# Layers 1 and 2 values by seven block products in a four-layer graph-attention stack, with the mask of layer 0 added out of PSUM

## The chip, the cores and the metric

The kernel runs on one core of one Trainium2 chip. The metric is the device time of one execution in microseconds (us). Three runs of the kernel before gave 2368.14, 2368.44 and 2372.44 us, the median is 2368.44 us.

## What is computed

The input is `x`, 32 graphs of 512 nodes with 256 features, and `adj`, a 0/1 adjacency of 512 x 512 for each graph. All is fp32. Four layers follow one another; each normalises its input, applies a graph attention, and adds the result back. Graphs are independent of one another.

```
for every layer:  h = relu(layernorm(x));  x = x + layer(h)
layer 0: s = (h att_W) h^T / 16 + mask(0 or -1000);  A = softmax(s)
         y = tanh(A (h W0 + b0));  out = tanh(A (y W1 + b1))
layer 1: Wh = h W^T;  e = leaky(Wh a1 [rows] + Wh a2 [columns]);  masked softmax;  out = A Wh
layer 2: Hh = h W;  e = exp(-leaky(s + d)) * (adj != 0);  out = elu(e Hh / rowsum)
layer 3: g = h W;  logits = g a12 g^T + g a1 + g a2;  leaky, masked softmax;
         out = elu(h W1 + A h W2)
```

"Values" in what follows are the rows that the attention averages: h W0 in layer 0, Wh in layer 1, Hh in layer 2, h W2 in layer 3. In layers 1 and 2 the two score columns (Wh a1 and Wh a2) are computed together with the values, as two further columns of the weights.

## The kernel before

**A graph as a list of operations.** A graph has 512 nodes: 4 tiles of 128 rows (NT = 4). `graph(b, ...)` does not emit instructions; it lists operations (`op`), each with an engine, a cost out of the table at L38 to L50, the operations it comes after, and the tiles that it uses. `Plan.order` (L131) is a list scheduler that runs all 32 lists through a simulation with due times. It fixes one order for each engine and gives the tiles their places: 34 SBUF pages (`PAGES`), 8 PSUM banks, 5 value buffers, 3 planes buffers, and `FLIGHT` slots, one for each graph in work. `SLACK` (L67) stretches the costs of VectorE, ScalarE and the DMAs in that simulation. `Plan.best` tries several spacings of the graphs' due times and keeps the one whose replay ends first. On the chip each engine then runs its list strictly in order, with semaphores where one engine needs another.

**One layer in the list.** `normed` (L521) computes mean and variance of each row on VectorE (L526, L527, L530), the reciprocal root on POOL (L533), the normed rows on ScalarE (L540). Then the rows are transposed by DMA: the fp32 words are split into two planes of 16 bits by a copy on VectorE (`split`, L545), the planes are turned by a DMA (L548), and a copy on ScalarE (`join`, L560) puts the halves back together as hT (features on partitions). Only layer 0 of graph 0 is turned by TensorE.

**Products.** In layers 0 (from graph 1 on) and 3 most products are made by a scheme of seven block products in place of eight (`seven`, L586). The operands are cut into 2 x 2 blocks; sums of blocks are formed on VectorE by `block_sums` (L618: four sums of 128 x 256 for each operand that isn't a weight; the sums of weights are made once by `seven_of`, L388). Each of the seven products then accumulates into a bank that is read out part by part: a product is added onto what the bank holds, a block is written out by one engine (`write`), the next product is added onto it, and three blocks get a further term by VectorE (`add`). So TensorE may enter the next product of a bank only when the block before has been read out. In layers 1 and 2 the values are made plainly by `scored_values` (L649): for each tile of 128 nodes, two products with 258 columns (2 scores and 256 values), and a copy out by ScalarE (L662). In the trace each fp32 product appears as two matmul records, so a layer has 4 tiles x 2 x 2 = 16 such records a graph.

**Scores of layer 0.** The seven products `q0` (L833) are read out by ScalarE (L847; the block (1,0) directly by the exponential, L841), added to by VectorE (L850), exponentiated by ScalarE (L841), and multiplied by `mask0` on VectorE (L856). `mask0` is 1 for an edge and 2^-100 for none (L516).

**Attention.** `attend` (L711) multiplies the weights e by the values, with a column of ones behind the values that yields the row sum: L721, 16 steps of 2 records for each pair of tiles, 257 columns in layers 0 to 2 and 259 in layer 3. Layers 1 to 3 add the result to x on VectorE: L929 in layer 1, and in layer 2 L962 and L966 for each tile of 128 x 256. Layer 0 has its own second product (L878, L896) and adds the result to x by L907.

Of the kernel before, what the change touches and what calls it, by code (L numbers as in the profile page):

```python
# [25 lines left out]
LEAST = 2.0**-126  # L26
LOWEST = -3.0e38
# [25 lines left out]
class Plan:  # L53
# [13 lines left out]
    SLACK = {"V": (1.05, 0.0), "A": (1.05, 0.0), "G": (1.5, 0.0), "D": (1.0, 800.0)}  # L67
# [138 lines left out]
def kernel(  # L206
# [36 lines left out]
    FLIGHT = 5  # L243
    PAGES, VALUES = 34, 5
    TURNED = 2
    LEAD = 2
# [105 lines left out]

    def transposed(w_sb, dst, after, *keys):
        done = []
        for c in range(HC):
            key = f"bank{next(banks)}"

            def turn(c, key):
                for r in range(HC):
                    nc.tensor.transpose(W[key][:, r * P : (r + 1) * P], w_sb()[:, r, c * P : (c + 1) * P], ident)  # L360

            def out_of(c, key):
                nc.vector.tensor_copy(dst()[:, c, :], W[key][:, : HC * P])

            a = prepare("PE", pe(nt=HC), after, partial(turn, c, key), key, *keys)
            done.append(prepare("V", V_ADD, [a], partial(out_of, c, key), key, *keys))
        return done
# [41 lines left out]
    l1_aug, l2_aug = (tile_of(n, H + 2) for n in ("l1_aug", "l2_aug"))  # L409
# [5 lines left out]
    for n, dst, w, key in (("w0", w0_s, w0, "raw9"), ("att", att_s, att_w, "raw10")):  # L415
# [9 lines left out]
    l3_wide = raw("raw8", H + 2)  # L425
    a = [load(l1_sb, rows_of(l1_w), "raw0")]
    ready["l1"] = transposed(l1_sb, lambda: l1_aug[:, :, 2:], a, "raw0")
    a += [load_column(l1_ac, l1_a.rearrange("n o -> (n o)"))]
    ready["l1"] += product(lambda d: l1_aug[:, d, 0:2], l1_sb,
                           lambda c: l1_ac.rearrange("p (o c) -> p c o", o=2)[:, c, :], 2, a, "raw0")  # L430
    a = [load(l2_aug[:, :, 2:], rows_of(l2_w))]
    a = ready["l2"] = a + transposed(lambda: l2_aug[:, :, 2:], l2_wt, a, "raw1")
    a = a + [load_column(l2_ac, l2_a.rearrange("o n -> (o n)"))]
    ready["l2"] = a + product(lambda d: l2_aug[:, d, 0:2], l2_wt,
                              lambda c: l2_ac.rearrange("p (o c) -> p c o", o=2)[:, c, :], 2, a, "raw1")
# [25 lines left out]
    def graph(b, adj_before, x_before):  # L461
# [53 lines left out]
        def mask0():  # L515
            nc.vector.tensor_scalar(T["mask0"], T["codeT"], HUGE, TINY, ALU.is_equal, ALU.max)  # L516
# [4 lines left out]
        def normed(l, xs):  # L521
# [21 lines left out]
            def split(t):  # L543
                bits = T[f"xn{l}"][:, t, :].bitcast(U16).rearrange("p (h b) -> p b h", b=2)
                nc.vector.tensor_copy(T[f"planes{l}_{t}"], bits)  # L545
# [18 lines left out]
            for g in range(NT // 2):  # L564
# [7 lines left out]
                for t in (2 * g, 2 * g + 1):  # L572
                    flat, over = f"planes{l}_{t}", f"planesT{l}_{t}"
                    a = op("A", A_NORM, [r], partial(norm, t), "x", f"xn{l}")
                    if b == l == 0:

                        key = f"bank_n{t}"
                        a = op("PE", pe(nt=2 * HC), [a], partial(turn_pe, t, key), f"xn{l}", key)
                        done.append(op("V", V_ADD, [a], partial(out_of, t, key), f"hT{l}", key))
                        continue  # L580
                    a = op("V", V_SPLIT, [a], partial(split, t), f"xn{l}", flat)
                    a = op("D", D_TURN, [a], partial(turn, t), flat, over)
                    done.append(op("A", A_JOIN, [a], partial(join, t), over, f"hT{l}"))
# [34 lines left out]
        def block_sums(dst, source, b, after, left):  # L618
# [16 lines left out]
            one = op("V", V_SUM, after, partial(form, 1), dst, source)  # L635
            three = op("V", V_SUM, after, partial(form, 3), dst, source)
# [12 lines left out]
        def scored_values(l, hs, w_aug, ready):  # L649

            cols = w_aug.shape[2]
            vs = []
            for t in range(NT):
                key = f"bank_v{l}{t}"

                def product(t, key):
                    for c in range(HC):
                        nc.tensor.matmul(T[key][:, :cols], T[f"hT{l}"][:, c, t * P : (t + 1) * P],  # L658
                                         w_aug[:, c, :], start=(c == 0), stop=(c == HC - 1))

                def values(t, key):
                    nc.scalar.copy(T[f"v{l}"][:, t, :cols], T[key][:, :cols])  # L662

                a = op("PE", pe(n258=4), [hs[t]] + ready, partial(product, t, key), key, f"hT{l}")
                vs.append(op("A", A_HALF, [a], partial(values, t, key), key, f"v{l}"))
            return vs

        def leaky_exp_t(l, vs, sign):
# [24 lines left out]
            def leaky(c):  # L693
                row = T[key] if turned else T[key][:, 0, :]
                nc.scalar.activation(e(l, c), row, AF.Prelu, bias=T[v][:, c, 1:2], alpha=ALPHA)  # L695
# [15 lines left out]
        def attend(l, es, vs, use):  # L711
# [3 lines left out]
            lead = LEAD if l < 3 else 0  # L715
# [12 lines left out]
            return done  # L728

# [80 lines left out]
        else:  # L810
# [29 lines left out]
            def exp0(i, l, key=None):  # L840
                nc.scalar.activation(block_e0(i, l), two_tiles(key, 0, N // 2) if key else block_e0(i, l), AF.Exp,  # L841
                                     scale=float(H) ** -0.5)

            def write_q(i, l, key, start, after):
                if (i, l) == (1, 0):
                    return op("A", A_COPY, after, partial(exp0, i, l, key), key, f"e0_{l}")
                return op("A", A_COPY, after, lambda: nc.scalar.copy(block_e0(i, l), two_tiles(key, 0, N // 2)), key, f"e0_{l}")  # L847

            def add_q(i, l, key, start, after):
                a = op("V", V_MASK, after, lambda: nc.vector.tensor_tensor(  # L850
                    block_e0(i, l), block_e0(i, l), two_tiles(key, 0, N // 2), ALU.add), key, f"e0_{l}")
                exps.append(op("A", A_EXP, [a], partial(exp0, i, l), f"e0_{l}"))
                return exps[-1]

            def masked0(i, l):
                nc.vector.tensor_tensor(block_e0(i, l), block_e0(i, l), T["mask0"][:, two(l), half(i)], ALU.mult)  # L856

            exps = []
            qb = seven("q0", pe(n256=4), lambda x, right_after=right_after, left_after=left_after: right_after(x) + left_after(x),
                       ("hT0", "hs0", "fa0", "fs0"), partial(scores0, right, left), write_q, add_q)  # L860
            es = {il: op("V", V_MASK, [a, m0], partial(masked0, *il), "mask0", f"e0_{il[1]}") for il, a in qb.items()}
# [27 lines left out]
        for g in range(NT // 2):  # L889
# [16 lines left out]
            def add_z(t):  # L906
                nc.vector.tensor_add(T["x"][:, t, :], T["x"][:, t, :], T["z0"][:, t, :])  # L907
# [4 lines left out]
            xs += [op("V", V_ADD, [a], partial(add_z, 2 * g + j), "z0", "x") for j in range(2)]  # L912
# [6 lines left out]
        vs = scored_values(1, hs, l1_aug, ready["l1"])  # L919
# [3 lines left out]
        def second(t, a, key):  # L923
            def sums():
                nc.vector.reciprocal(T["rs1"][:, t : t + 1], T[key][:, H : H + 1])

            def add():
                xt = T["x"][:, t, :]
                nc.vector.scalar_tensor_tensor(xt, T[key][:, :H], T["rs1"][:, t : t + 1], xt, ALU.mult, ALU.add)  # L929
# [8 lines left out]
        vs = scored_values(2, hs, l2_aug, ready["l2"])  # L938
# [7 lines left out]
        def third(t, a, key):  # L946
            def sums():
                rs = T["rs2"][:, t : t + 1]

                nc.vector.tensor_scalar(rs, T[key][:, H : H + 1], LEAST, None, ALU.max)  # L950
                nc.vector.reciprocal(rs, rs)


            def lower():
                nc.scalar.activation(T["y2"][:, t, :], T[key][:, :H], AF.Exp, scale=T["rs2"][:, t : t + 1])

            def upper():
                nc.scalar.activation(T["r2"][:, t, :], T[key][:, :H], AF.Relu, scale=T["rs2"][:, t : t + 1])

            def add_lower():  # L960
                xt = T["x"][:, t, :]
                nc.vector.scalar_tensor_tensor(xt, T["y2"][:, t, :], 1.0, xt, ALU.min, ALU.add)  # L962

            def add_upper():
                xt = T["x"][:, t, :]
                nc.vector.scalar_tensor_tensor(xt, T["r2"][:, t, :], -1.0, xt, ALU.add, ALU.add)  # L966

            a = op("V", V_TWO, [a], sums, key)
            l = op("A", A_TANH, [a], lower, key, "y2")
            u = op("A", A_TANH, [a], upper, key, "r2")  # L970
            l = op("V", V_ADD, [l], add_lower, "y2", "x")
            return op("V", V_ADD, [l, u], add_upper, "r2", "x")

        xs = attend(2, es, vs, third)


# [12 lines left out]
        def block_v(i, l):  # L989
            return T["v3"][:, two(l), i * (HALF + 1) : (i + 1) * (HALF + 1)]  # L990

        def write_v(i, l, key, start, after):
            return op("A", A_HALF, after, lambda: nc.scalar.copy(block_v(i, l), two_tiles(key, start, HALF + 1)), key, "v3")

        def add_v(i, l, key, start, after):
            return op("V", V_SUM, after, lambda: nc.vector.tensor_tensor(
                block_v(i, l), block_v(i, l), two_tiles(key, start, HALF + 1), ALU.add), key, "v3")

        vb = seven("v3", pe(nt=4), lambda x: right_after(x) + ready["l3"], ("hT3", "hs3"), partial(by_nodes, l3_aug, right), write_v, add_v)
# [84 lines left out]
        def fourth(t, a, key):  # L1084
# [3 lines left out]
            def both_terms():  # L1088
                p = T[key][:, : H + LEAD].rearrange("p (i k) -> p i k", i=2)[:, :, :HALF]
# [77 lines left out]
```

## Time and profile before

| what | us |
|---|---|
| median of three runs | 2368.44 |
| the profiled execution, its own time | 2372.2 |
| its span, first to last instruction | 2370.4 |
| TensorE busy with matmuls (mean clock granted 0.999) | 2347.1 |
| VectorE busy | 2029.9 |
| ScalarE busy | 1724.8 |
| POOL busy | 253.1 |

The profiled execution has 1.8 us outside its span and lies 3.8 us above the median of the runs. In the page and the tables PE is TensorE's matmuls, PEld its weight loads (they overlap the matmuls), DVE is VectorE, ACT is ScalarE. "L658" is line 658 of the kernel. A name such as `bank_v` stands for all buffers of that kind; `bank_a` is the attention's accumulator. A row of a group reads: line, engine, operation, output <- inputs, count, busy time, mean of one. A row of waits reads: engine and line that waited, what it waited for, us in total, times, longest. Matmuls are pipelined: the duration of one record is longer than the step to the next, and it is the step that a longer or shorter stream is made of.

### The profile page before, as it was taken

Reading aid. Unit: us, or ns where it says so; the run is one execution under the profiler, and the core shown is the slowest. Engines: PE = TensorE matmul, PEld = TensorE weight load, DVE = VectorE, ACT = ScalarE, POOL = GpSimd, SP = SyncE. Lnnn points to the kernel's source line nnn. Section 1 sums busy time; section 2 is a strip of 40 time slices with the busy share of each in tenths; the row PEclk is TensorE's granted clock in tenths of the full one; section 3 lists DMA queues with packets and bytes.
Section 4 is the critical chain, followed back from the end, with each engine's and each line's share of the span. In section 5 each row is a group of like instructions: output and inputs, shape, how many; then the busy total and the mean of one; then the engine's idle time right before and its main releaser. Section 6 shows DMA issues by size and latency. Waiting matters only on the chain.

```text
span 2370.4 us, 36184 instructions
## 1 busy us (share of the span) xinstructions
PE 2347.1 (99%) x11590; PEld 1985.5 (84%) x11590; DVE 2029.9 (86%) x6042; ACT 1724.8 (73%) x3386; POOL 253.1 (11%) x315
## 2 busy tenths in 40 slices
PE   7999999999999999999999999999999999999999
PEld 5788888888888888888888888888888888888888
DVE  6777888889888898888898888988888888888789
ACT  5577777777777777777777777777777777766785
POOL 3000100011100111101110001110011100101110
PEclk9999999999999999999999999999999999999999
DMA  7421332433333433324333234333243332422221
GB/s 189 92 54 35 86 74 67 88 81 72 79 67 79 94 64 82 72 68 92 75 76 78 66 82 89 67 81 70 70 94 67 81 81 67 99 49 50 47 49 44
DMA packets 432015, 178.71 MB, mean 75 GB/s; under 512 B 386288, under 2 KB 403824, under 8 KB 431824
## 3 DMA queue, kind: packets, MB, share of 16 engines
q1 hardware_dynamic: 426464, 158.03, 31.0%
q0 software_dynamic: 5216, 18.23, 2.3%
q8 instruction: 92, 1.51, 0.3%
q14 instruction: 99, 0.81, 0.1%
q10 hardware_dynamic: 144, 0.13, 0.0%
HBM read 67.64 MB, written 16.89 MB: 36 GB/s over the span
## 4 chain that ended last, share of the span: by engine, by line
PE 94%; DVE 3%; DMA 1%; ACT 1%; issue 0%; POOL 0%; SPq 0%; DVEq 0%; ACTq 0%; POOLq 0%
PE bank_a L721 36%; PE bank_z L878 9%; PE bank_v L658 9%; PE bank_o L896 5%; PE bank_s3p L1006 4%; PE bank_q0p L833 4%; PE bank_f3p L742 4%; PE bank_v0p L768 4%; PE bank_w3p L768 4%; PE bank_f0p L742 4%; PE bank_s3q L1006 3%; PE bank_q0q L833 3%; PE bank_v3p L768 2%; PE bank_v3q L768 2%; DMA planesT<-planes 1%; DVE st L526 0%
## 5 line engine op out<-in xcount | busy, mean ns | idle before, releaser
L721 PE MATMUL bank_a<-v,e 128*128 128x257 f32 (+1 forms) x4096 | 986.2, 381 | 5.1 <-DVE e L808 3.2
L721 PEld LDWEIGHTS bank_a<-v,e 128*128 128x128 f32 x4096 | 769.4, 190 | 164.6 <-issue 53.9
L560 ACT COPY hT<-planesT 128x512 uint16<-128x512 uint16 x508 | 378.2, 767 | 43.7 <-DMA planesT<-planes 43.3
L533 POOL TENSOR_TENSOR rstd<-ve,mhalf 128x2 f32<-128x2 f32 x256 | 218.3, 883 | 1668.7 <-DVE ve L530 1142.9
L540 ACT ACTIVATE xn<-x,off,rstd 128x256 f32<-128x256 f32 x512 | 276.2, 594 | 40.6 <-DVE off L536 39.8
L658 PE MATMUL bank_v<-l_aug,hT 128*128 128x258 f32 x1024 | 257.1, 381 | 1.0 <-ACT hT L560 0.8
L878 PE MATMUL bank_z<-e,y 128*128 128x512 f32 x512 | 240.6, 592 | 0.0
L545 DVE COPY planes<-xn 128x512 uint16<-128x512 uint16 x508 | 204.7, 416 | 20.6 <-DMA planesT<-planes 15.3
L658 PEld LDWEIGHTS bank_v<-l_aug,hT 128*128 128x128 f32 x1024 | 191.2, 190 | 28.4 <-ACT hT L560 1.4
L526 DVE BATCH_NORM_STATS2 st<-x 128x6 f32<-128x256 f32 x512 | 208.6, 407 | 4.3 <-DMA x<-in_x_dram 4.2
L1052 ACT ACTIVATE e<-e,zero 128x512 f32<-128x512 f32 x128 | 88.1, 717 | 96.5 <-DVE crest L1030 95.0
L695 ACT ACTIVATE e<-row,v 128x512 f32<-128x512 f32 x224 | 153.0, 715 | 4.5 <-DMA row<-row 4.3
L698 ACT ACTIVATE e<-e 128x512 f32<-128x512 f32 x256 | 156.2, 629 | 0.0
L662 ACT COPY v<-bank_v 128x258 f32<-128x258 f32 x256 | 95.9, 375 | 81.5 <-PE bank_v L658 79.8
L878 PEld LDWEIGHTS bank_z<-e,y 128*128 128x128 f32 x512 | 97.0, 190 | 68.0 <-issue 57.6
L869 ACT ACTIVATE y<-bank_a,rs 128x256 f32<-128x256 f32 x128 | 56.8, 470 | 83.0 <-DVE rs L866 83.0
L1013 DVE SCALAR_TENSOR_TENSOR e<-bank_s3p,v,mask 128x256 f32<-128x256 f32 x256 | 111.1, 475 | 6.5 <-PE bank_s3p L1006 6.3
L896 PE MATMUL bank_o<-w_sb,zT 128*128 128x256 f32 x512 | 116.1, 379 | 0.0
L896 PEld LDWEIGHTS bank_o<-w_sb,zT 128*128 128x128 f32 x512 | 97.0, 190 | 13.2
L527 DVE BATCH_NORM_AGGREGATE mv<-st 128x2 f32<-128x6 f32 x512 | 93.1, 182 | 17.5
L841 ACT ACTIVATE e<-e 128x512 f32<-128x512 f32 x93 | 58.5, 629 | 56.8 <-DVE e L850 56.8
L1058 ACT ACTIVATE e<-e 128x512 f32<-128x512 f32 x128 | 76.8, 634 | 18.5 <-DVE e L1055 18.5
(186 smaller groups left out, 4361.9 us busy)
## 6 DMA issues: line engine op xcount, KB each, us to landing
adj<-in_adj_dram SPq DMA_DIRECT2D x128, 256.0 KB, 2.9
x<-in_x_dram SPq DMA_DIRECT2D x31, 512.0 KB, 5.1
out_dram<-y POOLq DMA_DIRECT2D x31, 512.0 KB, 4.1
row<-row SPq DMA_DIRECT2D x56, 256.0 KB, 3.5
planesT<-planes SPq DMA_TRANSPOSE x508, 2.4
codeT<-code SPq DMA_TRANSPOSE x128, 2.5
crest<-crest SPq DMA_TRANSPOSE x64, 2.4
row<-sT SPq DMA_DIRECT2D x56, 2.0 KB
```

The costliest lines, as they stand in the source:

```text
L526: nc.vector.bn_stats(T[f"st{l}"][:, t, :], T["x"][:, t, :])
L533: nc.gpsimd.tensor_tensor(T[f"rstd{l}"][:, two(g)], T[f"ve{l}"][:, two(g)], mhalf[:, two(g)], ALU.pow)
L540: nc.scalar.activation(T[f"xn{l}"][:, t, :], T["x"][:, t, :], AF.Relu, bias=T[f"off{l}"][:, t : t + 1], scale=T[f"rstd{l}"][:, t : t + 1])
L545: nc.vector.tensor_copy(T[f"planes{l}_{t}"], bits)
L560: nc.scalar.copy(bits[:, :, :, t * P : (t + 1) * P], T[f"planesT{l}_{t}"].rearrange("p (b c) n -> p b c n", b=2))
L658: nc.tensor.matmul(T[key][:, :cols], T[f"hT{l}"][:, c, t * P : (t + 1) * P], w_aug[:, c, :], start=(c == 0), stop=(c == HC - 1))
L721: nc.tensor.matmul(T[key][:, : LEAD + H + 1 - lead], e(l, c)[:, t * P : (t + 1) * P], T[f"v{l}"][:, c, lead:], start=(c == 0), stop=(c == ...
L742: nc.tensor.matmul(p[:, : N // 2], w[:, x - 1, :], right(x), start=fresh, stop=True, skip_group_check=True)
L768: nc.tensor.matmul(p[:, j * k : (j + 1) * k], right(x)[:, j * P : (j + 1) * P], w[:, x - 1, :], start=fresh and j == 0, stop=True, skip_gr ...
L833: nc.tensor.matmul(p[:, j * N // 2 : (j + 1) * N // 2], right(x)[:, j * P : (j + 1) * P], left(x), start=fresh and j == 0, stop=True, skip ...
L878: nc.tensor.matmul(T[f"bank_z{k}"], T["y0"][:, c, k * P : (k + 1) * P], e(0, c), start=(c == 0), stop=(c == NT - 1))
L896: nc.tensor.matmul(T[key][:, j * H : (j + 1) * H], T["zT"][:, k, t * P : (t + 1) * P], w1_sb[:, k, :], start=(k == 0), stop=(k == HC - 1))
```

## The change

- **Values of layers 1 and 2 by seven products.** `scored_values` now calls `seven`, as the values of layer 3 did before (whose own functions it replaces). The weights have 2 x 129 columns, one score column ahead of each half of the values. Operands: `block_sums` of hT1 and hT2 (new tiles hs1, hs2), and `seven_of` of the two weights once at the start.
- **The order of the value columns.** The score of a row is column 0 and the other score column 129; attention in layers 1 and 2 starts at column 1 instead of 2 and streams 258 columns instead of 257, and the results are read in two runs of 128 (`product_of`).
- **Layer 0's mask.** From graph 1 on `mask0` is 0 for an edge and -1104 for none. VectorE writes a block of scores as the sum of the bank and mask0 (four of 128 x 512) in place of ScalarE's three copies; block (1,0) is then exponentiated from SBUF. The four products by mask0 are gone.
- **Pairs in one operation.** Two of the four sums of `block_sums` for hs0, hs1, hs2, hs3 become one of 512 elements (`form_two`); the additions to x at the end of layers 0 and 2 are done for two tiles at once.
- **Layer 1's split** into planes is a copy on ScalarE (`BYACT`).
- **Planner.** `FLIGHT` 6 instead of 5; `SLACK` 1.03 instead of 1.05 for VectorE and ScalarE.

```diff
-    SLACK = {"V": (1.05, 0.0), "A": (1.05, 0.0), "G": (1.5, 0.0), "D": (1.0, 800.0)}
+    SLACK = {"V": (1.03, 0.0), "A": (1.03, 0.0), "G": (1.5, 0.0), "D": (1.0, 800.0)}
...
-    FLIGHT = 5
+    FLIGHT = 6
+    BYACT = (1,)
...
-    l1_aug, l2_aug = (tile_of(n, H + 2) for n in ("l1_aug", "l2_aug"))
+    l1_aug, l2_aug = (tile_of(n, HALF + 1, 7) for n in ("l1_aug", "l2_aug"))
...
+    ready["l1"] = seven_of(l1_wide, l1_aug, HALF + 1, t, "raw11")
...
+    ready["l2"] = seven_of(l2_wide, l2_aug, HALF + 1, a, "raw12")
...
         def mask0():
-            nc.vector.tensor_scalar(T["mask0"], T["codeT"], HUGE, TINY, ALU.is_equal, ALU.max)
+            if b == 0:
+                nc.vector.tensor_scalar(T["mask0"], T["codeT"], HUGE, TINY, ALU.is_equal, ALU.max)
+            else:
+                nc.vector.tensor_scalar(T["mask0"], T["codeT"], HUGE, AWAY, ALU.not_equal, ALU.mult)
...
-                nc.vector.tensor_copy(T[f"planes{l}_{t}"], bits)
+                (nc.scalar.copy if l in BYACT else nc.vector.tensor_copy)(T[f"planes{l}_{t}"], bits)
...
-                    a = op("V", V_SPLIT, [a], partial(split, t), f"xn{l}", flat)
+                    a = op("A" if l in BYACT else "V", A_JOIN if l in BYACT else V_SPLIT, [a], partial(split, t), f"xn{l}", flat)
...
-            one = op("V", V_SUM, after, partial(form, 1), dst, source)
-            three = op("V", V_SUM, after, partial(form, 3), dst, source)
+            def form_two():
+                nc.vector.tensor_tensor(T[dst][:, 0:3:2, :], T[source][:, :, half(1)],
+                                        T[source][:, 0, :].rearrange("p (l n) -> p l n", l=2), ALU.subtract)
+
+            if left:
+                one = op("V", V_SUM, after, partial(form, 1), dst, source)
+                three = op("V", V_SUM, after, partial(form, 3), dst, source)
+            else:
+                one = three = op("V", V_MASK, after, form_two, dst, source)
...
-        def scored_values(l, hs, w_aug, ready):
...
-                a = op("PE", pe(n258=4), [hs[t]] + ready, partial(product, t, key), key, f"hT{l}")
-                vs.append(op("A", A_HALF, [a], partial(values, t, key), key, f"v{l}"))
-            return vs
+        def scored_values(l, after, right, w, ready):
...
+            def write(i, l_, key, start, after):
+                return op("A", A_HALF, after, lambda: nc.scalar.copy(block(i, l_), two_tiles(key, start, HALF + 1)),
+                          key, f"v{l}")
+
+            def add(i, l_, key, start, after):
+                return op("V", V_SUM, after, lambda: nc.vector.tensor_tensor(
+                    block(i, l_), block(i, l_), two_tiles(key, start, HALF + 1), ALU.add), key, f"v{l}")
+
+            return seven(f"v{l}", pe(nt=4), lambda x: after(x) + ready, (f"hT{l}", f"hs{l}"), partial(by_nodes, w, right),
+                         write, add)
...
-            lead = LEAD if l < 3 else 0
+            lead = (LEAD, 1, 1, 0)[l]
...
             def write_q(i, l, key, start, after):
+                a = op("V", V_MASK, after + [m0], lambda: nc.vector.tensor_tensor(
+                    block_e0(i, l), two_tiles(key, 0, N // 2), T["mask0"][:, two(l), half(i)], ALU.add),
+                    key, f"e0_{l}", "mask0")
                 if (i, l) == (1, 0):
-                    return op("A", A_COPY, after, partial(exp0, i, l, key), key, f"e0_{l}")
-                return op("A", A_COPY, after, lambda: nc.scalar.copy(block_e0(i, l), two_tiles(key, 0, N // 2)), key, f"e0_{l}")
+                    return op("A", A_EXP, [a], partial(exp0, i, l), f"e0_{l}")
+                return a
...
-            def masked0(i, l):
-                nc.vector.tensor_tensor(block_e0(i, l), block_e0(i, l), T["mask0"][:, two(l), half(i)], ALU.mult)
...
-            xs += [op("V", V_ADD, [a], partial(add_z, 2 * g + j), "z0", "x") for j in range(2)]
+            xs += [op("V", V_MASK, [a], partial(add_z, g), "z0", "x")] * 2
...
         hs = normed(1, xs)
-        vs = scored_values(1, hs, l1_aug, ready["l1"])
+        right_after, right = block_sums("hs1", "hT1", lambda j, l: T["hT1"][:, j, half(l)], hs, left=False)
+        vb = scored_values(1, right_after, right, l1_aug, ready["l1"])
...
+            a = op("V", V_MASK, [u[0] for u in us[two(g)]], partial(add_lower, g), "y2", "x")
+            xs += [op("V", V_MASK, [a] + [u[1] for u in us[two(g)]], partial(add_upper, g), "r2", "x")] * 2
```

## The prediction on record

> **What bounds the kernel now.** I read the page first (busy shares, slices), then the stretches table, TensorE's waits, and last the chain that ended last, for the step from one matmul record to the next.
>
> The page, and then the table by stretches (columns: stretch, its length, busy us of PE, PEld, DVE, ACT, POOL, granted clock, DMA share, GB/s):
>
> ```profile
> PE 2347.1 (99%) x11590; PEld 1985.5 (84%) x11590; DVE 2029.9 (86%) x6042; ACT 1724.8 (73%) x3386; POOL 253.1 (11%) x315
> PE   7999999999999999999999999999999999999999
> ```
> ```profile
> 600.00:745.20 145.20, 145.20 (x721) 123.48 (x720) 126.72 (x376) 108.11 (x213) 15.51 (x18) 1.00 0.35 77
> 745.20:890.40 145.20, 145.20 (x722) 123.52 (x721) 126.75 (x377) 108.10 (x214) 15.49 (x18) 1.00 0.35 77
> ```
> ```profile
> 2200.00:2300.00 100.00, 98.06 (x490) 82.55 (x489) 78.24 (x252) 80.84 (x166) 10.69 (x13) 1.00 0.22 44
> 2300.00:2340.00 40.00, 39.24 (x242) 35.82 (x241) 39.07 (x96) 24.56 (x51) 0.79 (x1) 1.00 0.18 40
> 2340.00:2371.00 31.00, 24.61 (x126) 21.20 (x124) 26.75 (x64) 15.40 (x26) 1.50 (x2) 0.98 0.22 65
> ```
>
> The pattern of the trace repeats every 145.2 us, two graphs; in it TensorE never stands still, at full clock. A graph costs 72.6 us of TensorE and nothing else sets the pace. VectorE is busy 126.7 of 145.2 (87.3%, 63.4 us a graph), ScalarE 108.1 (74.4%, 54.0 us). TensorE's whole idle time is 2370.4 - 2347.1 = 23.3 us: 9.3 at the start (the first normed rows), about 5 more by 100 us, 9.1 in the last 171 us (171.0 - 161.9), almost nothing between. TensorE's waits from 200 to 2300 us:
>
> ```profile
> PE bank_a L721 <- DVE e L942: 1.0, 1, 1.0
> PE bank_v L658 <- ACT hT L560: 0.8, 2, 0.6
> PE bank_a L721 <- DVE e L916: 0.5, 1, 0.5
> ```
>
> So a change is worth what it takes out of TensorE's record stream, if the other engines still deliver in time. The chain (start, us to the next piece, what) gives the true step of a record; the "mean ns" of a group (381 for 258 columns) holds pipeline overlap and is not its price:
>
> ```profile
> 1259.20 0.87 PE bank_v L658 x4
> 1260.08 0.45 PE bank_v3p L768 x4
> 1260.52 0.45 PE bank_v3q L768 x4
> 1260.97 0.45 PE bank_v0p L768 x4
> 1261.41 0.86 PE bank_s3p L1006 x4
> ```
> ```profile
> 2137.68 3.49 PE bank_v L658 x16
> 2141.17 0.43 PE bank_f3p L742 x2
> ```
>
> 258 columns: 3.49 / 16 = 0.218 us. 129 columns (bank_v3): (1260.97 - 1260.08) / 8 = 0.111 us. 257 columns: pieces of 12.14 us for 56 records, 0.217 us.
>
> **The change part by part: TensorE.** Values of layers 1 and 2, per layer and graph: out go 16 records of 258 columns, 3.49 us; in come seven products of 4 records of 129 columns, 28 x 0.1113 = 3.12 us. Saved 0.37 us, over 64 layer-graphs 23.9 us. The attention of these layers now streams 258 columns instead of 257: 64 records a graph, 2048 in all. From 0.218 - 0.217 it is 1.4 ns each, from the 512-column step (1.72 / 4 = 0.430, so 0.84 ns a column) 0.8 ns: 2.8 or 1.7 us, say 2.3. Net on the path: -21.6 us.
>
> Here a rule speaks against the change. The Trainium skill (TensorE: Matmul & The Clock Gate, Back-to-back issue gap) says that in a stream of weight load and matmul both set the spacing, and gives about 81 ns at 128 columns against 131 at 512: narrow matmuls are hardly cheaper. Scaled along that line, 129 columns cost 81/98 = 0.83 of 258, and 28 x 0.83 x 0.218 = 5.1 us replaces 3.49: +100 us in all. The rows of this case, fp32 and with the weight loads beside them, show 0.111 against 0.218, a ratio of 0.51. I take the rows.
>
> **VectorE.** Priced by the step between back-to-back operations: two 256-element sums in 0.75 us, 0.334 apart; four of L1055 in 2.49 us, 0.603 apart for 512 elements. Per graph: layer 1's four splits leave, -1.33; sums of hs1 and hs2, one of 512 and two of 256 each, +2.54; six additions into v1 and v2 (as L996, 420 ns, same step), +2.00; hs0 and hs3 take the pair in one, -0.13; the mask: four products by mask0 (682 ns) go and four sums out of PSUM (as L1021, 684 ns) come, 0; layer 0's residual in pairs -0.13, layer 2's -0.26. Sum +2.7 us a graph, 63.4 to 66.1 in a period of 72.6 - 0.68 = 71.9: 92% busy. It hides under TensorE; the cover is 5.8 us a graph. How full this engine can be: 39.07 of 40 us (97.7%) from 2300 to 2340, with TensorE at 98%.
>
> **ScalarE.** Four splits of 128x512 uint16 come. No row shows one here. Nearest are the joins (L560, 767 ns, same size and type) and the copy of as many floats (L847, 584 ns): 2.3 to 3.1 us, and I take the joins. Three copies of q0 leave (-1.75 us), one exponential reads SBUF instead of PSUM (629 against 599 ns); the value copies stay four of 258 elements (375 and 371 ns). Net +0.6 to +1.4 us: 55.4 of 71.9, 77%. Hidden; cost taken as 0. The wait for the three planes buffers (15.3 us in all at L545) goes in part to ScalarE's queue, with exponentials and joins behind it: between 0 and its layer's quarter, 4 us of an engine that idles 16 us a graph; 0 taken.
>
> **Waits.** Each of the 64 new sevens has six hand-overs in which TensorE may not go on before ScalarE has copied a block or VectorE has added one; behind a waiting matmul everything on TensorE is queued. The kernel has 221 such sevens now, 1326 hand-overs, and TensorE's idle time at their lines (L833, L742) is 2.2 us: 1.7 ns each. 384 more at that price: 0.7 us. The upper end is the saturated stretch 2300:2340, where 0.76 of 40 us were lost; see the second rival. I take 0.7. The first q0 block is now written by VectorE, so mask0 must be there earlier. In the timeline mask0 (L516) is made at 646.9 us and that graph's first q0 product starts at 665.1, first mask use 679.6: 18 us stand before the new wait, so 0; if they were gone, the write and the next q0 product behind it would wait for the transposes of the codes (2.5 us of waiting at L516 in the whole run). The queues of SyncE and POOL keep their number of transfers; one more weight load on POOL (0.74 us) and two seven_of blocks on VectorE (six operations of 0.29 us each) fall into the start, ahead of the first use at 71.6 us: 0.
>
> **Six in flight.** It does no work. A v3 seven runs from 1253.1 to 1270.2 us in the trace, 17 us, plus 1.3 us for its sums; the plain products of layers 1 and 2 (two graphs' worth of 16 records) spread over 15 us in the same stretch (1244.8 to 1260.1). A graph's way grows by perhaps 5 to 10 us per layer; a sixth graph offers another 72 us of it. The pages stay at 34 and the PSUM banks at 8. Price in the middle: 0, from -1 to +1.
>
> **Ends.** VectorE is full from 2300 us on, but with layer 3 of the last graphs, where it gains 0.07 us a graph. Layers 1 and 2 of the last three graphs lie before, where it has 22 us to spare. I take +0.5 for the drain and nothing for the start.
>
> Sum: -21.6 + 0.7 + 0.5 = -20.4 us. Profiled execution: span 2370.4 to 2350.0, time 2372.2 to 2351.8 with the 1.8 us around the span. The median of the runs shown, 2368.44, lies 3.8 below that execution; from it, 2348.0.
>
> **The rivals.** *Given back at the ends.* The last graphs' longer way through layers 1 and 2 finds no other work: 5 to 8 us in each of two layers, so up to +15: 2353 to 2363. For it: TensorE already loses 9.1 us there, and few graphs are left to fill in. Against: the three last graphs run side by side, and TensorE is at 98% until 2340.
>
> *Slower: VectorE becomes the bound of the steady stretch.* If the operations don't fit into the planned order as tightly as their steps say, VectorE sits at the 97.7% of 2300:2340 throughout, TensorE loses 0.76/40 = 1.9% of 2200 us, +42, and the gain turns into +20: 2389. It decides from 0.977 x 71.9 - 63.4 = 6.9 us of added work a graph on; I count 2.7. For it: an in-order engine that has to deliver sums, q0 blocks and additions. Against: the present stretch at 87% loses nothing.
>
> *It doesn't do what it says.* 129 columns cost more between other work than inside a seven: 0.125 us a record would take the gain away (2368). Against: the step is the same wherever the chain has such a piece.
>
> *More than counted.* Six in flight fill the 5 us before 100 us and part of the drain: down to 2341.
>
> **Numbers.** As summed, 2344 to 2352: 0.66. At the ends 0.17. Better than 2344: 0.07. No gain, within 0.2% (about what a measurement of this kernel can tell from no change): 0.04. Slower: 0.06. So faster 0.90. The range leaves out the last two and the outer edges: 2341 to 2361.
>
> **What would show it.** Right: period near 71.9 us a graph with TensorE without gaps; the value records of layers 1 and 2 at 0.111 us; VectorE near 92%. Wrong: waits of TensorE on the new write or add lines of more than some microseconds; a drain longer than 9 us of idle; splits on ScalarE far over 767 ns.

## The result, and the profile after

The changed kernel takes 2355.01 us (median of 5 runs, 2353.48 to 2357.89) against 2368.44 us (5 runs, 2367.40 to 2372.44): ratio on record 0.9941, 95% interval 0.9930 to 0.9953. A second comparison gave 2356.99 and 0.9945 (0.9932 to 0.9957). Over 49 runs on record the kernel before has a median of 2370.95 (2366.98 to 2373.40). So the change is worth 13 to 16 us. The forecast was 20.4 us, to 2348.0: the result lies in the stated range (2341 to 2361), and 3 us outside the part of it that stood for the sum (2344 to 2352).

The page of the changed kernel, and its table by stretches (columns as in the prediction):

```profile
PE 2327.2 (99%) x12358; PEld 1991.0 (85%) x12358; DVE 2101.1 (89%) x6055; ACT 1719.8 (73%) x3421; POOL 253.0 (11%) x316
PE   8999999999999999999999999999999999999999
```
```profile
600.00:1800.00 1200.00, 1199.44 (x6408) 1033.28 (x6407) 1089.17 (x3133) 894.12 (x1780) 127.47 (x149) 1.00 0.34 78
2200.00:2300.00 100.00, 94.12 (x532) 82.80 (x531) 94.47 (x280) 79.58 (x167) 11.66 (x13) 1.00 0.23 48
2300.00:2340.00 40.00, 39.67 (x229) 35.67 (x229) 38.67 (x89) 23.41 (x43) 0.75 (x1) 1.00 0.16 34
2340.00:2352.00 12.00, 6.62 (x35) 5.21 (x34) 8.02 (x20) 2.82 (x5) 0.75 (x1) 0.95 0.25 87
```

Steady part: TensorE still has no gaps worth naming (1199.44 of 1200), VectorE is at 90.8% (1089.17 of 1200). The difference is seen in the second row: between 2200 and 2300 us VectorE went from 78.24 to 94.47 and TensorE lost 5.9 us there, 1.9 before.

TensorE's waits of the changed kernel from 2100 us to the end:

```profile
PE bank_w3p L793 <- ACT w L1092: 2.5, 1, 2.5
PE bank_f3p L767 <- DVE hs L648: 1.9, 1, 1.9
PE bank_v2p L793 <- DVE fa L782: 0.8, 1, 0.8
PE bank_a L742 <- DVE e L940: 0.7, 2, 0.4
```

The two long ones, at 2266 and 2272 us, come right after the last attention of layer 2; what is left for TensorE then is layer 3 of the last graphs. The engines that TensorE waits for are not idle meanwhile: from 2260 to 2275 us VectorE is busy 14.69 of 15 us and ScalarE 14.46, and TensorE 10.45. In the kernel before the last attention of layer 2 ends at 2292 us. There the two engines are about as full, yet TensorE runs 29.00 of 30 us. First before, then after:

```profile
2275.00:2290.00 15.00, 14.00 (x62) 11.33 (x62) 14.55 (x54) 14.50 (x32) 2.95 (x4) 1.00 0.17 30
2290.00:2305.00 15.00, 15.00 (x100) 13.83 (x100) 14.79 (x54) 14.28 (x31) 3.20 (x5) 1.00 0.22 42
```
```profile
2260.00:2275.00 15.00, 10.45 (x54) 8.46 (x52) 14.69 (x46) 14.46 (x33) 1.69 (x2) 1.00 0.30 55
```

The new records in the chain (start, us to the next piece):

```profile
1291.18 0.86 PE bank_q0q L858 x4
1292.04 0.86 PE bank_s3p L1024 x4
1292.91 0.45 PE bank_v1p L793 x4
1293.35 0.87 PE bank_a L742 x4
```

Four records of 129 columns take 0.45 us between other work too, as in the rows before.

The way of a graph, from its first code operation on VectorE (here it takes a slot) to its store on POOL, is read from the timeline, first before (the eleventh graph), then after (the eleventh too):

```profile
628.50 0.68 DVE L505 TENSOR_SCALAR code<-adj 128x1024 bf16<-128x1024 int32 x1
...
964.18 0.79 POOL L1120 DMA_DIRECT2D out_dram<-y  x1 [14.16 <-DVE y L1103]
```
```profile
580.20 0.68 DVE L517 TENSOR_SCALAR code<-adj 128x1024 bf16<-128x1024 int32 x1
...
1000.88 0.79 POOL L1138 DMA_DIRECT2D out_dram<-y  x1 [11.29 <-DVE y L1121]
```

It grew from 335.7 to 420.7 us, that is from 4.6 to 5.8 periods. The graphs' order is a different one throughout, so this is not the delay of one layer, but how many graphs the planner keeps open. Two of the experiments below show it. e6, which has the plain values and six slots, has a way of 425.3 us; e3, which has the seven products and five slots, has 326.9 (the eleventh graph of e6, then of e3):

```profile
534.26 0.69 DVE L521 TENSOR_SCALAR code<-adj 128x1024 bf16<-128x1024 int32 x1
...
959.52 0.88 POOL L1194 DMA_DIRECT2D out_dram<-y  x1 [6.32 <-DVE y L1177]
```
```profile
630.84 0.69 DVE L521 TENSOR_SCALAR code<-adj 128x1024 bf16<-128x1024 int32 x1
...
957.77 0.79 POOL L1194 DMA_DIRECT2D out_dram<-y  x1 [10.54 <-DVE ve L549]
```

So the length of the way goes with the number of slots; that the seven products lengthen it is not shown by it.

**A ledger of TensorE.** In "busy" a short gap disappears, since the modelled end of a record lies beyond the next start. So I worked out from the starts of all records how much each step is over the step of its width (0.1108, 0.1116, 0.2161, 0.2169, 0.2178, 0.2186, 0.4290 us for 128, 129, 256, 257, 258, 259, 512 columns). The steps at these values are the work; what is over is lost, by waits or by stretches of half clock. Some 14 to 17 us lie ahead of the first record and behind the last. "Time" is the median of the runs; all other columns are of the one profiled execution, "before" and "changed" of the first one on record.

| kernel | time us | span | work | lost to 100 us | 100 to 2000 | after 2000 |
|---|---|---|---|---|---|---|
| before | 2368.4 | 2370.4 | 2336.7 | 10.6 | 2.4 | 5.5 |
| before again (e12) | 2370.0 | 2366.8 | 2336.7 | 7.5 | 2.2 | 5.6 |
| changed | 2355.0 | 2351.7 | 2315.5 | 7.4 | 3.5 | 11.4 |
| changed again (e1) | 2357.0 | 2353.7 | 2315.5 | 8.4 | 3.6 | 12.6 |
| five in flight (e2) | 2425.1 | 2424.3 | 2315.5 | 17.9 | 47.3 | 28.2 |
| seven alone (e3) | 2421.1 | 2413.2 | 2315.5 | 10.0 | 42.1 | 31.1 |
| plain values (e4) | 2395.0 | 2395.1 | 2338.5 | 10.8 | 16.9 | 13.8 |
| seven and six (e5) | 2377.7 | 2376.6 | 2315.5 | 10.1 | 16.0 | 18.4 |
| six alone (e6) | 2377.4 | 2374.5 | 2338.5 | 9.5 | 4.4 | 7.1 |
| split on VectorE (e7) | 2378.2 | 2376.7 | 2315.5 | 10.0 | 19.8 | 15.8 |
| mask by product (e8) | 2361.4 | 2357.1 | 2315.5 | 7.7 | 9.2 | 8.9 |
| masks twice (e9) | 2373.6 | 2371.8 | 2315.5 | 9.1 | 15.7 | 16.4 |
| slack 1.05 (e10) | 2371.8 | 2371.8 | 2315.5 | 10.4 | 18.5 | 12.9 |
| finer plan (e11) | 2354.1 | 2354.0 | 2315.5 | 8.9 | 8.1 | 6.7 |

From e12 to the changed kernel: work -21.2, start -0.1, steady +1.3, end +5.8, sum -14.2 of the 15.1 us between the spans; the rest lies ahead of the first record and behind the last.

### The profile page after: what moved, and what is told of

Read it like the earlier page. It is cut to its first block, busy times and chain, and to the rows that moved or that the text cites. A ratio compares the mean times of both kernels' runs of the same rounds, so it can differ in the third digit from the quotient of the medians.

```text
span 2351.7 us, 37549 instructions
## 1 busy us (share of the span) xinstructions
PE 2327.2 (99%) x12358; PEld 1991.0 (85%) x12358; DVE 2101.1 (89%) x6055; ACT 1719.8 (73%) x3421; POOL 253.0 (11%) x316
## 4 chain that ended last, share of the span: by engine, by line
PE 95%; DVE 4%; ACT 1%; DMA 0%; issue 0%; SPq 0%; POOL 0%; DVEq 0%; ACTq 0%
PE bank_a L742 37%; PE bank_z L902 9%; PE bank_o L920 5%; PE bank_s3p L1024 4%; PE bank_q0p L858 4%; PE bank_v0p L793 4%; PE bank_f3p L767 4%; PE bank_f0p L767 4%; PE bank_w3p L793 4%; PE bank_s3q L1024 3%; PE bank_q0q L858 3%; PE bank_v1p L793 2%; PE bank_v3p L793 2%; PE bank_v2p L793 2%; PE bank_v2q L793 2%; PE bank_v1q L793 2%
## 5 line engine op out<-in xcount | busy, mean ns | idle before, releaser
L742 PE MATMUL bank_a<-v,e 128*128 128x258 f32 (+2 forms) x4096 | 1022.4, 381 | 3.4 <-DVE e L833 2.4
L742 PEld LDWEIGHTS bank_a<-v,e 128*128 128x128 f32 x4096 | 744.5, 190 | 110.7 <-issue 17.5
L555 ACT ACTIVATE xn<-x,off,rstd 128x256 f32<-128x256 f32 x512 | 278.4, 593 | 43.3 <-DVE off L551 41.5
L560 DVE COPY planes<-xn 128x512 uint16<-128x512 uint16 x380 | 156.3, 420 | 17.9 <-ACT xn L555 9.5
L866 ACT ACTIVATE e<-e 128x512 f32<-128x512 f32 x124 | 77.8, 629 | 112.2 <-DVE e L869 58.2
L719 ACT ACTIVATE e<-e 128x512 f32<-128x512 f32 x256 | 157.4, 631 | 0.0
L679 ACT COPY v<-bank_v1p 128x258 f32<-128x258 f32 x128 | 47.7, 373 | 113.7 <-PE bank_v1p L793 112.8
L648 DVE TENSOR_TENSOR hs<-hT,hs 128x256 f32<-128x256 f32 x254 | 105.2, 414 | 0.9
L651 DVE TENSOR_TENSOR hs<-hT 128x512 f32<-128x512 f32 x127 | 86.5, 681 | 15.1 <-ACT hT L575 14.9
L869 DVE TENSOR_TENSOR e<-bank_q0p,mask 128x512 f32<-128x512 f32 x124 | 84.5, 681 | 16.8 <-PE bank_q0p L858 15.3
L679 ACT COPY v<-bank_v3p 128x258 f32<-128x258 f32 x128 | 47.8, 373 | 62.0 <-PE bank_v3p L793 61.0
```

What stands on the lines that cost most here:

```text
L555: nc.scalar.activation(T[f"xn{l}"][:, t, :], T["x"][:, t, :], AF.Relu, bias=T[f"off{l}"][:, t : t + 1], scale=T[f"rstd{l}"][:, t : t + 1])
L719: nc.scalar.activation(e(l, c), e(l, c), AF.Exp, scale=sign)
L742: nc.tensor.matmul(T[key][:, : LEAD + H + 1 - lead], e(l, c)[:, t * P : (t + 1) * P], T[f"v{l}"][:, c, lead:], start=(c == 0), stop=(c == ...
```

## The experiments

All kernels but e12 come from the changed one by switches and single lines, so their line numbers differ a little (L880 here is L858 of the changed kernel, L815 is L793). The planner makes a new order for each.

**e1, the changed kernel again** and **e12, the kernel before again.** No edit.

> The changed kernel once more, with nothing changed in what it does. It tells how far one profiled execution lies from another. If the 18.7 us between the two spans on record are what the change does, this gives a span of 2350 to 2354 us and a time around 2355. If the two profiled executions were by chance the high end of one kernel and the low end of the other, its span may be up to 2356 with the same sums of TensorE's records, and the difference lies in some single waits that the trace can name.

> The kernel before once more, for a second profiled execution: the one on record took 2372.2 us, the upper end of what its runs show (2366 to 2374). If single executions of the same list differ by a few waits of TensorE or stretches of lower clock, this one will show another sum of them: a span between 2365 and 2372.

e1: span 2353.7, 2356.99 us, 0.9945. e12: span 2366.8, 2370.02 us, 1.0003 (0.9994 to 1.0012). e12 loses 3.1 us less in the first 100 us than the execution on record, which had, among other things, a stretch of half clock at 31.6 us that e12 has not; the steady part and the end are the same within 0.2. So some 3 of the 18.7 us between the two spans on record were the start of one execution. e1 has the same waits as the changed kernel's first execution and one more stretch of half clock, of 3.4 us, just after the two long waits; the 2260 to 2280 us of the first execution, then of e1:

```profile
2260.00:2280.00 20.00, 15.45 (x83) 12.99 (x82) 18.90 (x63) 18.84 (x43) 3.38 (x4) 1.00 0.29 55
```
```profile
2260.00:2280.00 20.00, 15.67 (x75) 13.37 (x74) 18.74 (x64) 18.99 (x41) 2.77 (x4) 0.91 0.29 54
```

Both spans lie where they were expected. Single executions of one kernel lie 2 to 4 us apart, by what happens in the first 100 us and by stretches of half clock.

**e2, five in flight.**

```diff
-    FLIGHT = 6
+    FLIGHT = 5
```

> The changed kernel with five graphs in flight instead of six. Theory A, the prediction's: the sixth graph does no work and is worth -1 to +1 us, so 2353 to 2358 us. Theory B: a graph now takes longer from its codes to its store than five periods. In the traces on record that way is 336 us before and 417 to 423 us after; five periods of 72 us are 360 us. Then five in flight hold TensorE back: if the way shrinks half way to the old one, 378 us and some 20 us until the next graph begins, a period is about 80 us and the time 2500; if it shrinks to 360, some 2400. Anything from 2385 to 2520 speaks for B.

2425.13 us, ratio to before 1.0235 (1.0219 to 1.0250): 68 to 70 us above the changed kernel. Theory A, the prediction's, is out. Its TensorE waits, longest first:

```profile
PE bank_q0p L880 <- DVE e L899: 16.3, 26, 1.3
PE bank_n L572 <- ACT xn L559: 9.5, 2, 9.4
PE bank_f3p L789 <- ACT fa L799: 6.2, 2, 5.0
PE bank_q0p L880 <- DVE fs L652: 6.0, 2, 4.7
```

The first row is a hand-over of the new kind, a q0 block written by VectorE, 26 times. In the changed kernel the same row stands at 0.6 us. The time lies in Theory B's range, but that doesn't show its mechanism. The way of the eleventh graph is 358 us and it had begun 10.7 us after a slot came free, (358 + 11) / 5 = 73.8 us a graph; but way and free time together make up slots times period in every run, whatever causes the period.

**e3, seven products alone**, and **e5, seven products and six in flight.** Against the changed kernel:

```diff
-    SLACK = {"V": (1.03, 0.0), "A": (1.03, 0.0), "G": (1.5, 0.0), "D": (1.0, 800.0)}
+    SLACK = {"V": (1.05, 0.0), "A": (1.05, 0.0), "G": (1.5, 0.0), "D": (1.0, 800.0)}
...
-    FLIGHT = 6
+    FLIGHT = 5
...
-    BYACT = (1,)
+    BYACT = ()
```

The first two edits are e3's alone. In both, mask0 is multiplied after the exponential again, and the sums of blocks and the additions to x are made one by one, with the lines of the kernel before.

> The kernel before with one part of the change alone: values of layers 1 and 2 by seven products. Mask by multiplication, sums one by one, all splits on VectorE, five in flight. TensorE's work is that of the changed kernel, VectorE's is 4.7 us a graph above the kernel before (68 of 72 us, 95%). Theory A: TensorE stays covered, so about 2350 to 2356 us. Theory B, the way of a graph against five periods, adds VectorE as the busier engine: slower than before, 2385 to 2520 us.

> The kernel before with two parts of the change: values of layers 1 and 2 by seven products, and six graphs in flight with the planner's slack of 1.03. The parts that take work from VectorE or move it (mask out of PSUM, pairs, layer 1's split on ScalarE) are left out. VectorE has 68 of 72 us a graph. If in flight is what the seven products lacked, most of the 52 us between five and six come back, to 2355 to 2375 us, and what is left to 2355 is the price of VectorE's fuller list. If VectorE at 95% is the bound, it stays above 2395.

e3: 2421.10 us, 1.0213 (1.0196 to 1.0230). e5: 2377.68, 1.0031 (1.0019 to 1.0043). The 21 us of TensorE's work are saved in both, and lost again: e3 loses 83 us, e5 44, against 15 to 19 of the kernel before. Six in flight, with the slack that goes with it, is worth 43 us here. e5 missed its expected 2355 to 2375 by 3 us. One detail speaks against "slots" as the whole mechanism: in e3 a slot was free for 41 us before the next graph took it, with a way of 327 us. Fewer open graphs also leave the planner less to put into a gap. The two are not told apart: that the sixth slot is needed is shown, why is open.

**e6, six in flight alone** (with slack 1.03 and the new column order, so 258 columns in the attention of layers 1 and 2).

> The kernel before with six in flight and slack 1.03 and nothing else (the weights of layers 1 and 2 in the new order of columns, so 258 columns in their attention, 2 to 3 us of TensorE). If a sixth graph is worth something by itself, below 2366 us; if it only serves the longer way that the seven products make, 2368 to 2380, within some us of the kernel before plus those 2 to 3.

2377.36 us, 1.0028 (1.0019 to 1.0038). As the second case said: nothing gained by itself. The kernel before with slack 1.03 and five in flight was not run, so the slack's own part there is open.

**e4, plain values in the changed kernel**, with 258 columns and hT's tiles one by one.

```diff
-        vb = scored_values(1, right_after, right, l1_aug, ready["l1"])
-        vs = [tuple(vb.values())] * NT
+        vs = plain_values(1, hs, l1_aug, ready["l1"])
...
-        vb = scored_values(2, right_after, right, l2_aug, ready["l2"])
-        vs = [tuple(vb.values())] * NT
+        vs = plain_values(2, hs, l2_aug, ready["l2"])
```

`plain_values` is the old `scored_values`, and the two weights stay as they are loaded.

> The changed kernel with the values of layers 1 and 2 made plainly again (258 columns, no sums of blocks for these layers); all else stays: mask out of PSUM, pairs, layer 1's split on ScalarE, six in flight. Both theories give TensorE its 21 to 23 us back, and VectorE is at some 82%: 2372 to 2380 us. If it came out at or under 2362, the gain would be due to the other parts and not to the shorter stream of records.

2395.01 us, 1.0107 (1.0093 to 1.0121). The expectation failed by 15 us: work is up by 23.0 as counted, but TensorE loses 41.5 us, though VectorE is at 82%. Its largest wait is one for rows that are joined late on ScalarE:

```profile
PE bank_v L701 <- ACT hT L579: 11.4, 14, 1.5
```

e6, with the same values and without the other parts, loses 21. So no gain of the other parts is seen where the sevens are absent; but the 18 us between the two times are hardly more than what an order alone does (e10). Why the joins come late here was not tried.

**e7, layer 1's split on VectorE**, and **e9, layer 1's mask operations twice.**

```diff
-    BYACT = (1,)
+    BYACT = ()
```
```diff
         es = [op("V", V_MASK, [a], partial(masked1, c), "codeT", f"e1_{c // 2}") for c, a in enumerate(es)]
+        es = [op("V", V_MASK, [a], partial(masked1, c), "codeT", f"e1_{c // 2}") for c, a in enumerate(es)]
```

> The changed kernel with layer 1's split into planes back on VectorE: 1.3 us a graph more there (67.4 of 72), 2.5 less on ScalarE. By the prediction VectorE's work is covered and this costs nothing: 2353 to 2358 us. If the cover is thinner than its 5.8 us a graph, 2362 to 2375.

> The changed kernel with each of layer 1's four mask operations done twice (a maximum and minimum with the same values, so the second changes nothing): 2.4 us a graph more on VectorE, planned with its cost. It prices VectorE's room directly. By the prediction's cover (5.8 us a graph, bound only from 97.7%) it is free: 2353 to 2360 us. If the lists can't be packed beyond some 92% of VectorE, a graph costs 67.8/0.92 = 73.7 us, 1.6 more than now, so up to 50 us: 2370 to 2405.

e7: 2378.21 us, 1.0034 (1.0022 to 1.0046). e9: 2373.64, 1.0013 (1.0006 to 1.0019). Both lie 17 to 23 us over the changed kernel; "covered, so free" is wrong for the whole run. But e9's steady part shows where it is right:

```profile
600.00:1800.00 1200.00, 1198.59 (x6371) 1027.67 (x6370) 1112.01 (x3186) 895.14 (x1785) 139.61 (x150) 1.00 0.35 78
2200.00:2300.00 100.00, 93.76 (x514) 81.05 (x513) 94.03 (x275) 83.17 (x170) 10.46 (x12) 0.98 0.20 40
```

With VectorE at 92.7% TensorE still runs 1198.6 of 1200 us. Of e9's 15.7 us between 100 and 2000, 7.3 fall into 100 to 200; after 2000 it loses 5 more than the changed kernel. The 2.4 us a graph that e9 adds cost less than the 1.3 us that e7 adds, so the loss is no price per microsecond of VectorE.

**e10, the old slack.** No instruction differs.

```diff
-    SLACK = {"V": (1.03, 0.0), "A": (1.03, 0.0), "G": (1.5, 0.0), "D": (1.0, 800.0)}
+    SLACK = {"V": (1.05, 0.0), "A": (1.05, 0.0), "G": (1.5, 0.0), "D": (1.0, 800.0)}
```

> The changed kernel with the planner's slack for VectorE and ScalarE at the old 1.05. No instruction differs, only the order. If the order is a free choice, 2353 to 2358 us. If the slack counts as work when the lists are packed (2% of 66 us is 1.3 us a graph, as much as the split), it costs what the split on VectorE cost: 2365 to 2380.

2371.78 us, 1.0007 (1.0000 to 1.0014). The whole gain is gone by the order alone. The steady row of e10 (the changed kernel has 1199.44 and 1089.17 there):

```profile
600.00:1800.00 1200.00, 1197.49 (x6357) 1025.50 (x6356) 1079.93 (x3110) 892.16 (x1781) 137.38 (x150) 1.00 0.35 78
```

This bounds what every other experiment with a new order can say (e4 to e9): an order alone moves the time by 15 to 17 us. What e5, e7, e9 and e10 share is that VectorE's planned cost is 1.3 to 2.4 us a graph higher, in e10 without any work behind it, and that TensorE then loses 41 to 46 us in place of 22.

**e8, layer 0's mask by multiplication.**

```diff
             def write_q(i, l, key, start, after):
+                if (i, l) == (1, 0):
+                    return op("A", A_COPY, after, partial(exp0, i, l, key), key, f"e0_{l}")
+                return op("A", A_COPY, after, lambda: nc.scalar.copy(block_e0(i, l), two_tiles(key, 0, N // 2)), key, f"e0_{l}")
...
+            es = {il: op("V", V_MASK, [a, m0], partial(masked0, *il), "mask0", f"e0_{il[1]}") for il, a in es.items()}
```

> The changed kernel with layer 0's mask by multiplication again: ScalarE copies three blocks of scores out of PSUM (1.75 us a graph), VectorE multiplies four after the exponential; VectorE's sum is the same. By the prediction nothing changes: 2353 to 2358 us. If the shorter chain (no operation between exponential and attention) matters to the way of a graph, 2360 to 2370.

The cut shows the main lines; `mask0` too has its old values again. 2361.37 us, 0.9963 (0.9948 to 0.9977), 4 to 6 us over the changed kernel and in the range of the expectation's second case. By e10 that is within what an order does; whether the mask out of PSUM is worth anything by itself stays open.

**e11, a finer plan** for the changed kernel.

```diff
-    APART, APART_LAST = [1000.0 * k for k in range(32, 64, 2)], [1000.0 * k for k in (2, 8)]
+    APART, APART_LAST = [1000.0 * k for k in range(31, 36)], [1000.0 * k for k in (6, 8, 10, 12)]
...
-    SLACK = {"V": (1.03, 0.0), "A": (1.03, 0.0), "G": (1.5, 0.0), "D": (1.0, 800.0)}
+    SLACK = {"V": (1.005, 0.0), "A": (1.005, 0.0), "G": (1.5, 0.0), "D": (1.0, 800.0)}
```

> The changed kernel with slack 1.005 and a finer choice of the spacing of the graphs (steps of 1 us from 31 to 35, the last ones 6 to 12 us apart). Same instructions. TensorE's loss at the end (11.4 us after 2100 us in the changed kernel) is the part that another order may lower; the steady part loses only 2.7. If half of it comes back, 2348 to 2352 us; if tighter slack brings new waits, 2355 to 2365.

2354.10 us, 0.9935 (0.9922 to 0.9949), between the two ranges expected: no difference from the changed kernel that these runs can tell. The end is better as hoped (6.7 lost in place of 11.4), the steady part worse by 4.6:

```profile
600.00:1800.00 1200.00, 1198.26 (x6370) 1025.51 (x6369) 1077.89 (x3115) 898.34 (x1777) 117.52 (x148) 1.00 0.36 78
2200.00:2300.00 100.00, 97.37 (x565) 86.63 (x564) 96.17 (x287) 85.67 (x178) 10.47 (x14) 1.00 0.23 49
```

Here TensorE keeps 97.4 us with VectorE at 96%: a full VectorE alone does not make TensorE wait at the end, the order decides how much. Of the 5.8 us that the end lost more in the changed kernel than before, another order so won back 4.7.

## Why the prediction was right, and where it was not

**TensorE's stream: right.** -21.6 expected, -21.2 in the ledger: the values -23.0 (23.9 expected), the wider attention +1.8 (2.3), as the ledger of e6, with plain values and 258 columns, tells them apart. Every run with the sevens has this work, 2315.5 us. The trace's step of 0.111 us for 129 columns held; the Trainium skill's spacing (TensorE: Matmul & The Clock Gate, Back-to-back issue gap), taken as a ratio, would have made these products dearer than what they replace, and this fp32 kernel does not show it.

**"It hides under TensorE; the cover is 5.8 us a graph": right in the steady part.** 92% expected, 90.8% measured: VectorE's busy time rose by 71.2 us in all, 2.2 a graph where 2.7 was summed. The period is 72.05 us (the first code operations of the eleventh and the fifteenth graph lie at 580.2 and 868.4 us), 71.9 expected. TensorE's loss from 100 to 2000 us rose by 1.1 to 1.3 us, where I had 0.7 for the new hand-overs. The sums and writes cost what the rows said:

```profile
L651 DVE TENSOR_TENSOR hs<-hT 128x512 f32<-128x512 f32 x127 | 86.5, 681 | 15.1 <-ACT hT L575 14.9
L869 DVE TENSOR_TENSOR e<-bank_q0p,mask 128x512 f32<-128x512 f32 x124 | 84.5, 681 | 16.8 <-PE bank_q0p L858 15.3
L560 ACT COPY planes<-xn 128x512 uint16<-128x512 uint16 x128 | 75.1, 617 | 0.2 <-DMA planesT<-planes 0.2
```

The split on ScalarE takes 617 ns, between my two bounds (584 and 767) and below the one I took. (The two `seven_of` blocks are eight operations in the trace, not six; at 0.29 us each that changes nothing.)

**"I take +0.5 for the drain": the term that was mis-sized.** It is +5.8 (5.6 to 11.4; in e1 12.6). The step read VectorE's 22 us of room in 2200:2300 as cover for the last graphs' layers 1 and 2. But that room was a mean over 100 us. In the kernel before it lay ahead of 2275 us; from 2275 to 2305, about the end of layer 2, VectorE already stood at 29.3 of 30 us and ScalarE at 28.8. In the changed kernel the room filled (78 to 94%), and at the end of layer 2 TensorE lost 4.6 of 15 us waiting for these two full engines. Full engines alone don't explain it, since the kernel before and e11 have them too and lose little; what in the order makes the difference stays open. The sign that was named for this, a drain longer than 9 us of idle, came: 11.6 of the last 171 us, 9.1 before. The number of the rival "given back at the ends", 2353 to 2363, came true, at its lower edge. Its reason, a longer way that finds no other work, is not what the rows show, and e11 wins much of this loss back by the order.

**"Six in flight. It does no work. Price in the middle: 0": wrong.** Taken away it costs 68 to 70 us (e2), far more than the order alone in e10, and no run with five in flight shows the gain. The step compared a guessed 5 to 10 us per layer with a period of cover. Before, a way of 335.7 us in the 363 us of five slots left 27 us; that this was too little is not shown, since e3 had 41 us left and lost all the same. The sum survived this error only because the change brings the sixth slot with it.

**The planner's slack has no term in the sum at all.** e10 shows that with the old slack, and no instruction changed, the gain is 0: the prediction, 2341 to 2361, would have been missed by 11 us. That the order of the changed kernel was one of the good ones is luck as far as the prediction goes.

**Where a stall goes when cover is gone.** I priced the parts one by one, the split, the waits for buffers and the sixth slot at nothing. In the runs they are not separable: seven alone +50 us, six alone +6, both +7, with the split left out +7, with the old slack +1, all of it -14 to -16 (against 2371).

**The slower rival,** VectorE as bound from 97.7%, was not reached; 92.7% in the steady part (e9) did not reach the point either. "It doesn't do what it says" is out: the records have the price of the trace.

## What to carry to other kernels

When the bounding engine's work is cut by a scheme with more hand-overs, try it together with one more item in flight: here the seven products alone cost 50 us, the sixth slot alone 6, and the gain came only with both and the right order. Count the gain from steps between starts. Read the cover of the last items in short stretches: 22 us of room in 100 us were none in the 30 that mattered. Where a planner orders the work, test a part's worth beside a run that changes the order alone, since that alone moved this kernel by 15 to 17 us.

## What the runs showed of the hardware that I had not expected

TensorE's clock fell to half for 3.4 or 6.8 us after gaps shorter than I had expected to matter. In e1 two waits of 2.3 and 2.0 us within some 8 us were followed by 3.4 us of half clock; in the first execution of the same list, with waits of 2.5 and 1.9 us at the same place, they were not. In e2 a wait of 1.7 us at 2260 us, with one of 0.7 us 4 us earlier, stands beside 6.8 us of half clock (the row's mean clock is 0.91):

```profile
2240.00:2280.00 40.00, 36.14 (x205) 31.75 (x204) 32.49 (x98) 34.73 (x71) 5.37 (x6) 0.91 0.27 58
```

Over the whole of e2 the mean granted clock is 0.992. Its stretches of half clock ahead of the last record add up to 37.6 us, so that at most 19 of its 93 lost us are theirs. So gaps cost this kernel a second time, and not in every execution.
